# A paged-attention layer: new keys transposed on VectorE and moved through DRAM, score columns ordered by chunk, one mask buffer

## The chip, the cores and the metric

The kernel runs on one core of a Trainium2 chip. The metric is the device time of one execution in microseconds; three executions of the kernel before took 1196.81, 1202.33 and 1201.21 us, with a median of 1201.21. A further execution was taken under the hardware profiler; every line of a profile quoted here comes from such an execution.

## The reference

All data are fp32. There are B = 8 sequences of S = 128 tokens and width 512. Two layers with residuals are computed:

```python
x = x + einsum('bsi,boi->bso', x, weight[adapter_ids])       # one 512 x 512 adapter per sequence
q = rope(rmsnorm(x @ Wq.T, q_norm_w))    # 32 query heads of D = 128
k = rope(rmsnorm(x @ Wk.T, k_norm_w))    # 8 key heads: the "new keys"
v = x @ Wv.T
k_all = concat(k_cache[block_table], k)  # 512 cached keys, then 128 new ones
v_all = concat(v_cache[block_table], v)
scores = einsum('bqhd,bkhd->bhqk', q, k_all) * SCALE   # each key head serves 4 query heads
scores = where(valid, scores, -1e30)     # cached keys from cache_seqlens on are masked; new ones never
o = einsum('bhqk,bkhd->bqhd', softmax(scores), v_all)
x = x + o @ Wo.T
```

So every query head of every sequence has a 128 x 640 score matrix, and there are 256 of them.

## The kernel before, in words

The work is cut into 32 steps, `steps = [(g, b) ...]`: four groups g of 8 query heads with 2 key heads each (G = 4, GQ = 8, GK = 2), and in each group the eight sequences b. A step has eight heads h; heads 0 to 3 use the first key head (j = 0) and the first half of the queries (n = 0), heads 4 to 7 the second ones. The order of instructions on each engine is the order in which the Python code issues them: the tile scheduler is put into manual mode, and the pools (`work` with one buffer, `news` with three, and so on) only decide which buffer an allocation waits for.

For a head the loop issues two score matmuls into one PSUM buffer of two (`sc`, line 1031): 512 columns and 128 columns[...]. Line 1041 (VectorE) adds the mask while it copies the scores to `p` and keeps the minimum; line 1057 (ScalarE) takes the exponential with its sum; line 1098 (VectorE) inverts the sum; line 1105 (GpSimd, called POOL in the profile) scales `p`. `turn_p` (line 871, VectorE) transposes `p` in blocks of 32 x 32, `send` writes it to DRAM (`xp`), and `receive` reads it back as `pT`, which completes the transposition of 128 x 640.

Between the heads stand the pieces of `main`, matmuls of 512 columns: the projections of the next step (`pj_kv`, `pj_q`, from `project`), the values of the step before (`o`, from `values`), the output projection (`out`), and in group 0 the adapters (`y`). A planner deals them out: a matmul costs `UNIT = 0.86`, a TensorE transposition `TR = 0.11`, and each head gets an even share of what is left. Transpositions on TensorE that must stand at a certain head are entered in `turns_at` by `at(step, head, early, function, count)`; an early one is issued before the head's exponential, another after the pieces of the head.

Cached keys come by indirect DMA, are transposed by VectorE in `send_k` (line 786), go to DRAM (`xk`) and come back as `kT[j]` in `receive_k` (line 799). Queries go the same way in `send_q`: VectorE transposition `tq` (line 807), DRAM (`xq`, line 809), and back as `qT[n]` (line 816). All of these DMAs are issued on SP's queue in program order.

The new keys go another way. `rotate` normalises and rotates them into the tile `k` (for steps after the first GpSimd writes them with the features permuted, line 671, so that their feature order is that of the cached keys); `norm_scales` scales them on VectorE (line 695). `turn_k(i, j)` then transposes one key head on TensorE (`kt`, line 763), and ScalarE copies the result into the fifth chunk of `kT[j]` (line 764). This happens twice a step: for j = 0 at head 6 of the step before, and for j = 1 at head 2 of its own step. Queries of the first and last steps, listed in `by_pe`, are turned on TensorE in a like way (`turn_q`).

The tile `kT[j]` is laid out as (a, c, i): a is the key number modulo 4, c the chunk of 128 keys, i the index within. The score columns have this order, so both score matmuls read contiguous columns. The mask has the same order, in two buffers that steps use in turn (line 632).

Of the kernel before, what the change touches and what calls it, by code (L numbers as in the profile page):

```python
# [11 lines left out]
FP = mybir.dt.float32  # L12
# [6 lines left out]
P = 128  # L19
# [33 lines left out]
def lora_then_paged_attention(  # L53
# [155 lines left out]
    for a in range(4):  # L209
# [7 lines left out]
        )  # L217
        nc.gpsimd.memset(quad[rows, :], float(a))

    key_no = const.tile([P, 4, LC, Q4], FP, name="key_no")  # L220
    nc.gpsimd.iota(
        key_no,
        pattern=[[1, 4], [P, LC], [4, Q4]],
        base=0,
        channel_multiplier=0,
        allow_small_or_imprecise_dtypes=True,
    )
    mhalf = const.tile([P, GQ + GK], FP, name="mhalf")
    nc.gpsimd.memset(mhalf, -0.5)
    masks = [const.tile([P, 4, NC, Q4], FP, name=f"mask_{n}") for n in range(2)]  # L230
    for m in masks:
        nc.gpsimd.memset(m[:, :, LC, :], 0.0)


    lora_ix = const.tile([P, B], I32, name="lora_ix")
# [21 lines left out]
    for i, (g, b) in enumerate(steps):  # L257
        if i == 0:
            at(i, 2, False, lambda: turn_q(0, 1))
            at(i, 7, False, lambda: turn_q(1, 0))  # L260
            for n, h in enumerate((7, 8, 9, 10)):
                at(i, h, False, lambda n=n: turn_weights(("o1", 0, n)))
        if i == last:
            at(i - 1, 6, False, lambda: turn_q(last, 0))
            at(i, 2, True, lambda: turn_q(last, 1))
        at(i, 2, True, lambda i=i: turn_k(i, 1), 1)
        if i < last:
            at(i, 6, False, lambda i=i: turn_k(i + 1, 0), 1)
        if g == 0 and b + 2 < B:
            at(i, 0, True, lambda b=b: turn_x(b + 2))  # L270
            for c in range(KC):
                at(i, c if i else c + 2, False, lambda b=b, c=c: turn_lora(b + 2, c))
            at(i, 8 if i else 9, True, lambda b=b: turn_x1(b + 2))
    for turns in turns_at.values():
        turns.sort(key=lambda t: not t[0])

# [111 lines left out]
    def rope_angles():  # L388
        nc.vector.tensor_copy(row_f[:, 0:B], row_i[:, 0:B])
        row = spread(0)  # L390
        nc.vector.tensor_copy(len_f, row[:, 0:B])
        par_f = rope["par"] = const.tile([P, 1], FP, name="par_f")
        nc.vector.tensor_copy(par_f, par)
        pos = const.tile([P, B], FP, name="pos")
        nc.vector.tensor_scalar(pos, len_f, par_f, None, ALU.add)
        def temp(tag):
            t = work.tile([P, 4, D], FP, tag=tag, name=f"rope_{tag}")
            return t.rearrange("p h (u d) -> p (h u) d", u=2)

        ang, turns, sin, cos = temp("q0"), temp("q1"), temp("tq0"), temp("sw")  # L400
        nc.vector.tensor_tensor(
            ang,
            pos.unsqueeze(2).to_broadcast([P, B, H2]),
            row[:, at_ivf : at_ivf + H2].unsqueeze(1).to_broadcast([P, B, H2]),
            ALU.mult,
        )
        nc.vector.tensor_scalar(turns, ang, 1.0 / (2 * math.pi), ROUND, ALU.mult, ALU.add)
        nc.vector.tensor_scalar(turns, turns, ROUND, None, ALU.subtract)
        for part in (TWO_PI_1, TWO_PI_2, TWO_PI_3):
            nc.vector.scalar_tensor_tensor(  # L410
                out=ang, in0=turns, scalar=-part, in1=ang, op0=ALU.mult, op1=ALU.add
            )
        nc.vector.tensor_scalar(ang, ang, PI_BELOW, -PI_BELOW, ALU.min, ALU.max)
        rope.update(ang=ang, sin=sin, cos=cos)
# [185 lines left out]
    class Step:  # L600
        def __init__(self):
            self.kT, self.qT, self.q, self.pT, self.oT = {}, {}, {}, {}, {}
            self.scaled = set()

    st = [Step() for _ in steps]
# [22 lines left out]

    def make_mask(i):

        b = steps[i][1]
        nc.vector.tensor_scalar(
            masks[i % 2][:, :, 0:LC, :], key_no, len_f[:, b : b + 1], FAR, ALU.is_ge, ALU.mult
        )


# [2 lines left out]
    def rotate(i, y, dst, ss, table, n, between=None):  # L639
# [9 lines left out]
        sw = work.tile([P, 4, D], FP, tag="sw", name=f"sw_{i}_{table}")  # L649


        turned_order = i > 0 and (table == 1 or (i, n) in by_pe)
        cw = dst
        if turned_order and table:
            cw = sw[:, 2 : 2 + heads, :]
        elif turned_order:
            cw = work.tile([P, 4, D], FP, tag=f"tq{n}", name=f"cw_{i}_{n}")
        nc.vector.tensor_tensor(
            cw, t, CW[:, table, b, :].unsqueeze(1).to_broadcast([P, heads, D]), ALU.mult
        )  # L660
# [20 lines left out]
    def norm_scales(i, n, width):  # L681

        s = st[i]
        ss = s.ss[n]
        rs = small.tile([P, 6], FP, tag=f"rs{n}", name=f"rs_{i}_{n}")
        nc.gpsimd.tensor_scalar(ss[:, 0:width], ss[:, 0:width], EPS, 1.0, ALU.add, ALU.mult)
        nc.gpsimd.tensor_tensor(rs[:, 0:width], ss[:, 0:width], mhalf[:, 0:width], ALU.pow)  # L687

        def rest():
            for h in range(4):  # L690
                q = s.q[n][:, h, :]
                nc.scalar.activation(q, q, AF.Identity, scale=rs[:, h : h + 1])  # L692
            if n == 0:
                for j in range(GK):
                    nc.vector.tensor_scalar(
                        s.k[:, j, :], s.k[:, j, :], rs[:, 4 + j : 5 + j], None, ALU.mult
                    )
            s.scaled.add(n)
            if (i, n) not in by_pe:
                later.append(lambda: send_q(i, n))  # L700

        pending.append(rest)

    def project(i, what):
# [1 line left out]
        s = st[i]  # L706

        def after_kv(y):
            s.k = work.tile([P, GK, D], FP, tag="k", name=f"k_{i}")
            s.vn = news.tile([P, GW], FP, tag="vn", name=f"vn_{i}")  # L710
            s.ss = [
                small.tile([P, 6], FP, tag=f"ss{n}", name=f"ss_{i}_{n}") for n in range(2)
# [1 line left out]

            def rest():
                nc.scalar.copy(s.vn, y[:, GW : 2 * GW])
                rotate(i, y, s.k, s.ss[0][:, 4:6], 1, 0)

            pending.append(rest)

        def after_q(n):
            def after(y):
                s.q[n] = work.tile([P, 4, D], FP, tag=f"q{n}", name=f"q_{i}_{n}")

                def rest():
                    rotate(
                        i,
                        y,
                        s.q[n],
                        s.ss[n][:, 0:4],  # L730
                        0,
                        n,
# [14 lines left out]
    def turn_kc(i, j, copy=None):  # L747

        s = st[i]
        s.kT[j] = work.tile([P, 4, NC, Q4], FP, tag=f"kT{j}", name=f"kT_{i}_{j}")  # L750
        t = ps_mm.tile([P, HID], FP, tag="mm", name=f"kct_{i}_{j}")
        t = t.rearrange("d (c a i) -> d c a i", c=LC, a=4)
        for c in range(LC):
            nc.tensor.transpose(
                t[:, c, :, :].rearrange("d a i -> d (a i)"), s.kc[:, c, j * D : (j + 1) * D], ident
            )
        (copy or nc.scalar.copy)(s.kT[j][:, :, 0:LC, :].rearrange("d a c i -> d c a i"), t)

    def turn_k(i, j, copy=None):
        s = st[i]  # L760
        t = ps_mm.tile([P, HID], FP, tag="mm", name=f"kt_{i}_{j}")
        t = t[:, 0:P].rearrange("d (i a) -> d i a", a=4)
        nc.tensor.transpose(t.rearrange("d i a -> d (i a)"), s.k[:, j, :], ident)  # L763
        (copy or nc.scalar.copy)(s.kT[j][:, :, LC, :].rearrange("d a i -> d i a"), t)  # L764

    def turn_q(i, n, copy=None):
        s = st[i]
# [27 lines left out]

    def receive_k(i, j):
        s = st[i]
        s.kT[j] = work.tile([P, 4, NC, Q4], FP, tag=f"kT{j}", name=f"kT_{i}_{j}")
        nc.sync.dma_start(
            out=s.kT[j][:, :, 0:LC, :].rearrange("d b c k -> d b (c k)"),  # L800
            in_=s.xk[:, :, j, :].rearrange("b d x -> d b x"),
        )

    def send_q(i, n):
        s = st[i]
        tq = work.tile([P, 4, 4, Q4], FP, tag=f"tq{n}", name=f"tq_{i}_{n}")
        nc.vector.transpose(tq, s.q[n].rearrange("p h (a d) -> p a h d", a=4))
        xq = xch.tile([4, P, 4, Q4], FP, tag=f"xq{n}", name=f"xq_{i}_{n}")
        nc.sync.dma_start(
            out=xq.rearrange("b (i a) h q -> (b i) (a h q)", a=4),  # L810
            in_=tq.rearrange("p a h q -> p (a h q)"),
# [2 lines left out]
        def receive():  # L814
            s.qT[n] = work.tile([P, 4, 4, Q4], FP, tag=f"qT{n}", name=f"qT_{i}_{n}")
            nc.sync.dma_start(
                out=s.qT[n].rearrange("d b h q -> d b (h q)"),
                in_=xq.rearrange("b d h q -> d b (h q)"),
            )

        to_read.append((now[0], 0, receive))

# [45 lines left out]
    def turn_p(u, r):  # L868
        if r == 0:
            u.tp = turned.tile([P, 4, REP, QK], FP, tag="tp", name=f"tp_{u.i}_{u.j}")  # L870
        nc.vector.transpose(u.tp[:, :, r, :], u.p.pop(r).rearrange("q (a k) -> q a k", a=4))  # L871

    def turn_p_pe(u, r):

# [97 lines left out]
        turn_lora(1, c, on_vec if c % 2 else on_act, True)  # L972
    gather_lora(2)
    turn_q(0, 0, on_act)
    turn_k(0, 0, on_act)
    for _ in range(3):
        load_next()

# [2 lines left out]
    for i, (g, b) in enumerate(steps):  # L981
# [38 lines left out]
        for h in range(8):  # L1020
# [6 lines left out]
                )  # L1027

            sc = ps_sc.tile([P, 1024], FP, tag="sc", name=f"sc_{i}_{h}")
            for lo, hi in ((0, L), (L, LA)):  # L1030
                nc.tensor.matmul(  # L1031
                    sc[:, lo:hi],
                    lhsT=s.qT[j][:, r, :, :].rearrange("d h q -> d (h q)"),
                    rhs=s.kT[j].rearrange("d a c i -> d (a c i)")[:, lo:hi],
                    start=True,
                    stop=True,
                )
# [3 lines left out]
            nc.vector.tensor_tensor_reduce(  # L1041
                out=p,
                in0=sc[:, 0:LA],
                in1=masks[i % 2].rearrange("p a c i -> p (a c i)"),
                scale=1.0,
                scalar=3.0e38,
                op0=ALU.add,
# [52 lines left out]
            if i == last and j == 1:  # L1100

                unit.p[r] = probs.tile([P, LA], FP, tag="p", name=f"pk_{h}")
                p = p.rearrange("q (a c i) -> q a c i", a=4, c=NC)
                q = unit.p[r].rearrange("q (c i a) -> q a c i", a=4, c=NC)
            nc.gpsimd.tensor_scalar(q, p, unit.rc[:, one], 1.0, ALU.mult, ALU.mult)  # L1105
            prev = (unit, r)

# [75 lines left out]
```

## Time and profile before

| what | value |
|---|---|
| runs, median (lowest to highest) | 1201.21 us (1196.81 to 1202.33) |
| profiled execution, its own time | 1197.03 us |
| its span, first to last instruction | 1194.7 us |
| busy: TensorE, its weight loads, VectorE, ScalarE, GpSimd | 99%, 48%, 61%, 44%, 56% |
| granted TensorE clock | 1.0 |
| DMA queues, share of 16 engines | 59.6% (SP), 12.4% (ScalarE), 10.1% (GpSimd) |
| moved by DMA | 328.02 MB in 187148 packets |

The page names groups by line, engine and operation, as "out<-in", with partitions x elements, the count, the busy time in us and the mean duration of one in ns, and after a bar the idle time ahead of it on its engine and who ended it. PE is TensorE, PEld its weight loads, DVE VectorE, ACT ScalarE. A matmul of fp32 data appears as two passes, each with its own record, and a TensorE transposition as one. The records of neighbouring passes overlap in time, so that the distance between two starts, not the duration, is what a pass takes of TensorE.

### The profile page before, as it was taken

To read this page: it belongs to the slowest core of one execution; us is meant where nothing else is said; L and a number is where in the kernel's file an instruction comes from. 1 tells how busy PE (TensorE), PEld (TensorE's weight loads), DVE (VectorE), ACT (ScalarE), POOL (GpSimd) and SP (SyncE) were. 2 spreads that over 40 slices of the span, in tenths; PEclk is the share of its full clock that TensorE was granted. 3 is DMA by queue.
4 is the path that set the end of the run, shared out by engine and by line. 5 is a ranking of instruction groups with operands and counts; after the bars stand their busy time and mean duration, and the time that the engine had idled before them with its cause. 6 is when DMAs were issued, how large, how long until landed. Compare 5 with 4: busy or idle time off the path is not lost.

```text
span 1194.7 us, 12971 instructions
## 1 busy us (share of the span) xinstructions
PE 1178.0 (99%) x3412; PEld 576.4 (48%) x3412; DVE 733.6 (61%) x1675; ACT 531.5 (44%) x1648; POOL 674.9 (56%) x781
## 2 busy tenths in 40 slices
PE   7899999999999999999999999999999999999998
PEld 4554455454444444444444444444444444444454
DVE  5566656665566666766566676666657655565651
ACT  4564444444444444444444444444444444444432
POOL 5566455545566556555655556565556556655540
PEclk9999999999999999999999999999999999999999
DMA  8388788877988988888998998888898987777761
GB/s 290 110 278 273 261 292 293 275 261 246 309 289 301 334 303 300 294 270 300 296 303 280 340 313 298 298 278 300 267 319 277 303 285 264 243 255 242 260 222 60
DMA packets 187148, 328.02 MB, mean 275 GB/s; under 512 B 13124, under 2 KB 106052, under 8 KB 178116
## 3 DMA queue, kind: packets, MB, share of 16 engines
q1 hardware_dynamic: 124272, 239.23, 59.6%
q10 hardware_dynamic: 49524, 48.12, 12.4%
q0 software_dynamic: 13280, 39.86, 10.1%
q8 instruction: 27, 0.44, 0.2%
q14 instruction: 45, 0.37, 0.1%
HBM read 195.04 MB, written 132.12 MB: 274 GB/s over the span
## 4 chain that ended last, share of the span: by engine, by line
PE 97%; DMA 1%; ACT 1%; DVE 0%; POOL 0%; issue 0%; ACTq 0%; DVEq 0%; POOLq 0%
PE o L559 23%; PE sc L1031 23%; PE pj_q L559 18%; PE out L559 18%; PE pj_kv L559 9%; PE y L559 2%; PE lw L474 1%; DMA w_q<-xw_q 1%; PE x L474 1%; PE kt L763 1%; PE wt_q L492 0%; PE wt_kv L492 0%; PE qt L772 0%; PE wt_o L492 0%; PE pt L881 0%
## 5 line engine op out<-in xcount | busy, mean ns | idle before, releaser
L1041 DVE CUSTOM_DVE_ANT_0 p<-sc,mask 128x640 f32<-128x640 f32 x256 | 210.9, 824 | 400.5 <-PE sc L1031 400.4
L1057 ACT ACTIVATE p<-p,mn 128x640 f32<-128x640 f32 x256 | 211.6, 827 | 324.6 <-DVE mn L1041 322.4
L1031 PE MATMUL sc<-kT,qT 128*128 128x512 f32 (+1 forms) x1024 | 318.4, 433 | 1.1 <-ACT kT L764 0.8
L1105 POOL TENSOR_SCALAR p<-p,rc 128x640 f32<-128x640 f32 x252 | 201.9, 801 | 183.0 <-DVE rc L1098 181.0
L1031 PEld LDWEIGHTS sc<-kT,qT 128*128 128x128 f32 x1024 | 189.9, 190 | 226.4 <-issue 206.0
L559 PE MATMUL pj_q<-w_q,x1T 128*128 128x512 f32 x512 | 236.9, 593 | 1.4 <-ACT w_q L493 0.7
L559 PE MATMUL o<-pT,vc 128*128 128x512 f32 x512 | 236.9, 593 | 0.0
L559 PE MATMUL out<-w_o,oT 128*128 128x512 f32 (+1 forms) x528 | 234.9, 580 | 0.9 <-ACT oT L838 0.7
L871 DVE STREAM_TRANSPOSE tp<-p 128x640 f32<-128x640 f32 x252 | 211.0, 837 | 4.9 <-POOL p L1105 4.7
L610 POOL DMA_INDIRECT kc<-in_L_cond_k_cache_dram,key_ix x128 | 130.8, 1022 | 32.7 <-issue 32.5
L610 POOL DMA_INDIRECT vc<-in_L_cond_v_cache_dram,val_ix x128 | 127.9, 999 | 31.0 <-issue 30.8
L692 ACT ACTIVATE q<-q,rs 128x128 f32<-128x128 f32 x256 | 81.9, 390 | 139.1 <-POOL q L679 134.5
L559 PEld LDWEIGHTS out<-w_o,oT 128*128 128x128 f32 x528 | 95.7, 190 | 93.5 <-issue 89.9
L559 PEld LDWEIGHTS pj_q<-w_q,x1T 128*128 128x128 f32 x512 | 92.4, 190 | 93.8 <-issue 91.4
L559 PEld LDWEIGHTS o<-pT,vc 128*128 128x128 f32 x512 | 91.9, 190 | 88.6 <-issue 81.3
L559 PE MATMUL pj_kv<-w_kv,x1T 128*128 128x512 f32 x256 | 116.6, 593 | 0.7 <-ACT x1T L476 0.7
L671 POOL TENSOR_TENSOR k<-sw 128x256 f32<-128x256 f32 x31 | 22.9, 739 | 157.1 <-PE kt L763 133.4
L679 POOL TENSOR_TENSOR q<-q,sw 128x512 f32<-128x512 f32 x59 | 74.7, 1266 | 45.0 <-DVE sw L662 44.9
L646 ACT ACTIVATE sq<-pj_q 128x128 f32<-128x128 f32 x256 | 70.8, 277 | 50.4 <-PE pj_q L559 41.5
L687 POOL TENSOR_TENSOR rs<-ss,mhalf 128x6 f32<-128x6 f32 x64 | 77.6, 1212 | 5.3
L559 PEld LDWEIGHTS pj_kv<-w_kv,x1T 128*128 128x128 f32 x256 | 45.9, 190 | 45.6 <-issue 44.7
L559 PE MATMUL o<-pT,vn 128*128 128x512 f32 x128 | 65.4, 593 | 0.0
(123 smaller groups left out, 873.6 us busy)
## 6 DMA issues: line engine op xcount, KB each, us to landing
xp<-tp SPq DMA_DIRECT2D x63, 1280.0 KB, 5.9
pT<-xp SPq DMA_DIRECT2D x63, 1280.0 KB, 7.0
xk<-tk SPq DMA_DIRECT2D x31, 512.0 KB, 7.5
kT<-xk SPq DMA_DIRECT2D x62, 256.0 KB, 6.6
xq<-tq SPq DMA_DIRECT2D x59, 256.0 KB, 4.6
qT<-xq SPq DMA_DIRECT2D x59, 256.0 KB, 5.2
st_q<-in_L_cond_Wq_dram ACTq DMA_DIRECT2D x24, 256.0 KB, 5.3
xw_q<-tw_q ACTq DMA_DIRECT2D x24, 256.0 KB, 4.4
```

The source lines that it names most:

```text
L474: nc.tensor.transpose(t[:, j, :], blk, ident)
L559: nc.tensor.matmul(y[0], lhsT=lhsT, rhs=rhs, start=(k == 0), stop=(k == len(pieces) - 1))
L610: nc.gpsimd.indirect_dma_start(out=dst[:, c, :], out_offset=None, in_=src, in_offset=bass.IndirectOffsetOnAxis(ap=rows[:, g, at : at + 1], ...
L646: nc.scalar.activation(sq, t[:, h, :], AF.Square, scale=float(D) ** -0.5, accum_out=ss[:, h : h + 1])
L679: add.tensor_tensor(dst, cw, sw[:, 0:heads, :], ALU.add)
L687: nc.gpsimd.tensor_tensor(rs[:, 0:width], ss[:, 0:width], mhalf[:, 0:width], ALU.pow)
L692: nc.scalar.activation(q, q, AF.Identity, scale=rs[:, h : h + 1])
L871: nc.vector.transpose(u.tp[:, :, r, :], u.p.pop(r).rearrange("q (a k) -> q a k", a=4))
L1031: nc.tensor.matmul(sc[:, lo:hi], lhsT=s.qT[j][:, r, :, :].rearrange("d h q -> d (h q)"), rhs=s.kT[j].rearrange("d a c i -> d (a c i)")[:, ...
L1041: nc.vector.tensor_tensor_reduce(out=p, in0=sc[:, 0:LA], in1=masks[i % 2].rearrange("p a c i -> p (a c i)"), scale=1.0, scalar=3.0e38, op0 ...
L1057: nc.scalar.activation(p, p, AF.Exp, bias=unit.mn[:, one], scale=-1.0, accum_out=unit.sm[:, one])
L1105: nc.gpsimd.tensor_scalar(q, p, unit.rc[:, one], 1.0, ALU.mult, ALU.mult)
```

## The change

The new keys of a step are no longer transposed on TensorE, but for steps 0, 1 and the last. They are written beside the first four query heads, into a tile `q0` of 4 + GK heads; `send_q` transposes all six heads in one VectorE instruction and writes them to DRAM in one DMA, and a further DMA brings the keys back as `kn`, a tile of its own with three buffers. `kT[j]` keeps the four cached chunks alone. In steps 0, 1 and last, `turn_k` transposes both key heads on TensorE into one PSUM tile and copies them into `kn` at once.

The score columns are now ordered (c, a, i), chunk first. The 512-column matmul reads `kT[j]` in that order, as runs of 32 floats. The 128-column matmul reads `kn`, whose keys lie in natural order within each block b of 32, as (a, b, m): every fourth float. The mask and the key numbers follow the new order, the transposition of `p` reads runs of 32 floats and writes as before, and there is one mask buffer. For the last sequence of group 0 the entry of `turn_x1` is moved from the head after step 5 to its last head.

```diff
-    key_no = const.tile([P, 4, LC, Q4], FP, name="key_no")
+    key_no = const.tile([P, LC, 4, Q4], FP, name="key_no")
...
-    masks = [const.tile([P, 4, NC, Q4], FP, name=f"mask_{n}") for n in range(2)]
+    mask = const.tile([P, NC, 4, Q4], FP, name="mask")
...
         if i == 0:
             at(i, 2, False, lambda: turn_q(0, 1))
+            at(i, 6, False, lambda: turn_k(1), 2)
             at(i, 7, False, lambda: turn_q(1, 0))
...
         if i == last:
+            at(i - 1, 6, False, lambda: turn_k(last), 2)
             at(i - 1, 6, False, lambda: turn_q(last, 0))
             at(i, 2, True, lambda: turn_q(last, 1))
-        at(i, 2, True, lambda i=i: turn_k(i, 1), 1)
-        if i < last:
-            at(i, 6, False, lambda i=i: turn_k(i + 1, 0), 1)
...
-            at(i, 8 if i else 9, True, lambda b=b: turn_x1(b + 2))
+            at(i, (7 if b + 3 == B else 8) if i else 9, True, lambda b=b: turn_x1(b + 2))
...
-        turned_order = i > 0 and (table == 1 or (i, n) in by_pe)
+        turned_order = i > 0 and (i, n) in by_pe
...
-                    nc.vector.tensor_scalar(
-                        s.k[:, j, :], s.k[:, j, :], rs[:, 4 + j : 5 + j], None, ALU.mult
-                    )
+                    k = s.q[0][:, 4 + j, :]
+                    nc.vector.tensor_scalar(k, k, rs[:, 4 + j : 5 + j], None, ALU.mult)
...
-            s.k = work.tile([P, GK, D], FP, tag="k", name=f"k_{i}")
+            s.q[0] = work.tile([P, 4 + GK, D], FP, tag="q0", name=f"q_{i}_0")
...
-    def turn_k(i, j, copy=None):
-        s = st[i]
-        t = ps_mm.tile([P, HID], FP, tag="mm", name=f"kt_{i}_{j}")
-        t = t[:, 0:P].rearrange("d (i a) -> d i a", a=4)
-        nc.tensor.transpose(t.rearrange("d i a -> d (i a)"), s.k[:, j, :], ident)
-        (copy or nc.scalar.copy)(s.kT[j][:, :, LC, :].rearrange("d a i -> d i a"), t)
+    def new_keys(i):
+        s = st[i]
+        if s.kn is None:
+            s.kn = news.tile([P, 4, GK, Q4], FP, tag="kn", name=f"kn_{i}")
+        return s.kn
+
+    def turn_k(i, copy=None):
+        s = st[i]
+        t = ps_mm.tile([P, HID], FP, tag="mm", name=f"kt_{i}")
+        for j in range(GK):
+            nc.tensor.transpose(t[:, j * P : (j + 1) * P], s.q[0][:, 4 + j, :], ident)
+        (copy or nc.scalar.copy)(
+            new_keys(i).rearrange("d b j q -> d j b q"),
+            t[:, 0 : GK * P].rearrange("d (j b q) -> d j b q", j=GK, b=4),
+        )
...
     def send_q(i, n):
         s = st[i]
-        tq = work.tile([P, 4, 4, Q4], FP, tag=f"tq{n}", name=f"tq_{i}_{n}")
+        heads = 4 if n else 4 + GK
+        tq = work.tile([P, 4, heads, Q4], FP, tag=f"tq{n}", name=f"tq_{i}_{n}")
         nc.vector.transpose(tq, s.q[n].rearrange("p h (a d) -> p a h d", a=4))
-        xq = xch.tile([4, P, 4, Q4], FP, tag=f"xq{n}", name=f"xq_{i}_{n}")
+        xq = xch.tile([4, P, heads, Q4], FP, tag=f"xq{n}", name=f"xq_{i}_{n}")
...
-                in_=xq.rearrange("b d h q -> d b (h q)"),
+                in_=xq[:, :, 0:4, :].rearrange("b d h q -> d b (h q)"),
             )
+            if n == 0:
+                nc.sync.dma_start(
+                    out=new_keys(i).rearrange("d b j q -> d b (j q)"),
+                    in_=xq[:, :, 4 : 4 + GK, :].rearrange("b d j q -> d b (j q)"),
+                )
...
-        nc.vector.transpose(u.tp[:, :, r, :], u.p.pop(r).rearrange("q (a k) -> q a k", a=4))
+        nc.vector.transpose(
+            u.tp[:, :, r, :].rearrange("q a (c i) -> q a c i", c=NC),
+            u.p.pop(r).rearrange("q (c a i) -> q a c i", c=NC, a=4),
+        )
...
-            for lo, hi in ((0, L), (L, LA)):
+            for lo, hi, keys in (
+                (0, L, s.kT[j].rearrange("d a c i -> d c a i")),
+                (L, LA, s.kn[:, :, j, :].rearrange("d b (m a) -> d a b m", a=4)),
+            ):
                 nc.tensor.matmul(
                     sc[:, lo:hi],
                     lhsT=s.qT[j][:, r, :, :].rearrange("d h q -> d (h q)"),
-                    rhs=s.kT[j].rearrange("d a c i -> d (a c i)")[:, lo:hi],
+                    rhs=keys,
...
-                in1=masks[i % 2].rearrange("p a c i -> p (a c i)"),
+                in1=mask.rearrange("p c a i -> p (c a i)"),
```

More of the change, by code (lines that the diff above doesn't have):

```diff
@@ L218, in lora_then_paged_attention @@
         nc.gpsimd.memset(quad[rows, :], float(a))
-    key_no = const.tile([P, 4, LC, Q4], FP, name="key_no")
+    key_no = const.tile([P, LC, 4, Q4], FP, name="key_no")
     nc.gpsimd.iota(
         key_no,
-        pattern=[[1, 4], [P, LC], [4, Q4]],
+        pattern=[[P, LC], [1, 4], [4, Q4]],
         base=0,
@@ L229, in lora_then_paged_attention @@
     nc.gpsimd.memset(mhalf, -0.5)
-    masks = [const.tile([P, 4, NC, Q4], FP, name=f"mask_{n}") for n in range(2)]
-    for m in masks:
-        nc.gpsimd.memset(m[:, :, LC, :], 0.0)
+    mask = const.tile([P, NC, 4, Q4], FP, name="mask")
+    nc.gpsimd.memset(mask[:, LC, :, :], 0.0)
     lora_ix = const.tile([P, B], I32, name="lora_ix")
@@ L396, in temp @@
         def temp(tag):
-            t = work.tile([P, 4, D], FP, tag=tag, name=f"rope_{tag}")
-            return t.rearrange("p h (u d) -> p (h u) d", u=2)
+            n = 4 + GK if tag in ("q0", "tq0") else 4
+            t = work.tile([P, n, D], FP, tag=tag, name=f"rope_{tag}")
+            return t[:, 0:4, :].rearrange("p h (u d) -> p (h u) d", u=2)
         ang, turns, sin, cos = temp("q0"), temp("q1"), temp("tq0"), temp("sw")
@@ L602, in __init__ @@
             self.kT, self.qT, self.q, self.pT, self.oT = {}, {}, {}, {}, {}
+            self.kn = None
             self.scaled = set()
@@ L632, in make_mask @@
         nc.vector.tensor_scalar(
-            masks[i % 2][:, :, 0:LC, :], key_no, len_f[:, b : b + 1], FAR, ALU.is_ge, ALU.mult
+            mask[:, 0:LC, :, :], key_no, len_f[:, b : b + 1], FAR, ALU.is_ge, ALU.mult
         )
@@ L656, in rotate @@
         elif turned_order:
-            cw = work.tile([P, 4, D], FP, tag=f"tq{n}", name=f"cw_{i}_{n}")
+            cw = work.tile([P, 4 if n else 4 + GK, D], FP, tag=f"tq{n}", name=f"cw_{i}_{n}")
+            cw = cw[:, 0:4, :]
         nc.vector.tensor_tensor(
@@ L716, in rest @@
                 nc.scalar.copy(s.vn, y[:, GW : 2 * GW])
-                rotate(i, y, s.k, s.ss[0][:, 4:6], 1, 0)
+                rotate(i, y, s.q[0][:, 4 : 4 + GK, :], s.ss[0][:, 4:6], 1, 0)
             pending.append(rest)
@@ L722, in after @@
             def after(y):
-                s.q[n] = work.tile([P, 4, D], FP, tag=f"q{n}", name=f"q_{i}_{n}")
+                if n:
+                    s.q[n] = work.tile([P, 4, D], FP, tag=f"q{n}", name=f"q_{i}_{n}")
                 def rest():
@@ L728, in rest @@
                         y,
-                        s.q[n],
+                        s.q[n][:, 0:4, :],
                         s.ss[n][:, 0:4],
@@ L749, in turn_kc @@
         s = st[i]
-        s.kT[j] = work.tile([P, 4, NC, Q4], FP, tag=f"kT{j}", name=f"kT_{i}_{j}")
+        s.kT[j] = work.tile([P, 4, LC, Q4], FP, tag=f"kT{j}", name=f"kT_{i}_{j}")
         t = ps_mm.tile([P, HID], FP, tag="mm", name=f"kct_{i}_{j}")
@@ L756, in turn_kc @@
             )
-        (copy or nc.scalar.copy)(s.kT[j][:, :, 0:LC, :].rearrange("d a c i -> d c a i"), t)
-    def turn_k(i, j, copy=None):
+        (copy or nc.scalar.copy)(s.kT[j].rearrange("d a c i -> d c a i"), t)
+    def new_keys(i):
         s = st[i]
-        t = ps_mm.tile([P, HID], FP, tag="mm", name=f"kt_{i}_{j}")
-        t = t[:, 0:P].rearrange("d (i a) -> d i a", a=4)
-        nc.tensor.transpose(t.rearrange("d i a -> d (i a)"), s.k[:, j, :], ident)
-        (copy or nc.scalar.copy)(s.kT[j][:, :, LC, :].rearrange("d a i -> d i a"), t)
+        if s.kn is None:
[10 more added lines that the diff above has]
+        )
     def turn_q(i, n, copy=None):
@@ L797, in receive_k @@
         s = st[i]
-        s.kT[j] = work.tile([P, 4, NC, Q4], FP, tag=f"kT{j}", name=f"kT_{i}_{j}")
+        s.kT[j] = work.tile([P, 4, LC, Q4], FP, tag=f"kT{j}", name=f"kT_{i}_{j}")
         nc.sync.dma_start(
-            out=s.kT[j][:, :, 0:LC, :].rearrange("d b c k -> d b (c k)"),
+            out=s.kT[j].rearrange("d b c k -> d b (c k)"),
             in_=s.xk[:, :, j, :].rearrange("b d x -> d b x"),
@@ L974, in lora_then_paged_attention @@
     turn_q(0, 0, on_act)
-    turn_k(0, 0, on_act)
+    turn_k(0, on_act)
     for _ in range(3):
@@ L1102, in lora_then_paged_attention @@
                 unit.p[r] = probs.tile([P, LA], FP, tag="p", name=f"pk_{h}")
-                p = p.rearrange("q (a c i) -> q a c i", a=4, c=NC)
-                q = unit.p[r].rearrange("q (c i a) -> q a c i", a=4, c=NC)
+                p = p.rearrange("q (c a i) -> q c a i", a=4, c=NC)
+                q = unit.p[r].rearrange("q (c i a) -> q c a i", a=4, c=NC)
             nc.gpsimd.tensor_scalar(q, p, unit.rc[:, one], 1.0, ALU.mult, ALU.mult)
```

## The prediction

> **What bounds the kernel now.** I read the page's chain of waits first: who holds the end.
>
> ```profile
> PE 97%; DMA 1%; ACT 1%; DVE 0%; POOL 0%; issue 0%; ACTq 0%; DVEq 0%; POOLq 0%
> PE o L559 23%; PE sc L1031 23%; PE pj_q L559 18%; PE out L559 18%; PE pj_kv L559 9%; PE y L559 2%; PE lw L474 1%; DMA w_q<-xw_q 1%; PE x L474 1%; PE kt L763 1%; PE wt_q L492 0%; PE wt_kv L492 0%; PE qt L772 0%; PE wt_o L492 0%; PE pt L881 0%
> ```
>
> TensorE alone. Its own waits, asked for next, add up to 13.4 us in the whole span, 11.3 of them in the first 75 us; the steady part keeps 0.7 us of pj_kv for the copy into x1T and 0.5 and 0.2 us of pj_q where a new group's weights arrive. So a TensorE instruction taken out is worth its slot, one that gets longer costs its lengthening, and work on other engines counts only once TensorE has to wait for it. A busy PE is not the slot, since matmuls overlap; the slot is read from the timeline of TensorE, as the distance of starts:
>
> ```profile
> 620.59 2.74 PE L559 MATMUL out<-w_o,oT 128*128 128x512 f32 x6
> 623.17 0.27 PE L763 MATMUL kt<-ident,k 128*128 128x128 f32 x1
> 623.28 1.25 PE L1031 MATMUL sc<-kT,qT 128*128 128x512 f32 x4
> 624.36 3.60 PE L559 MATMUL out<-w_o,oT 128*128 128x512 f32 x8
> ```
>
> The x4 of sc are one head: a 512-column and a 128-column matmul, two passes each. Six 512-column passes take 623.17 - 620.59 = 2.58 us, 0.43 each; the head takes 624.36 - 623.28 = 1.08, so its 128-column passes have (1.08 - 0.86) / 2 = 0.107 to 0.11; the kt transposition 0.11. That is 0.84 ns a column in each. I use 0.1075.
>
> The third view is the groups with their shapes kept apart, for the price of a read or a write that steps over 16 bytes:
>
> ```profile
> L1031 PE MATMUL sc<-kT,qT 128*128 128x128 f32 x512 | 98.3, 274 | 0.0
> L763 PE MATMUL kt<-ident,k 128*128 128x128 f32 x64 | 17.4, 273 | 0.0
> ...
> L807 DVE STREAM_TRANSPOSE tq<-q 128x512 f32<-128x512 f32 x59 | 39.6, 670 | 0.0
> L786 DVE STREAM_TRANSPOSE tk<-kc 128x512 f32<-128x512 f32 x62 | 39.1, 670 | 0.0
> L506 DVE STREAM_TRANSPOSE tw_q<-st_q 128x512 f32<-128x512 f32 x24 | 25.5, 1061 | 0.0
> ...
> L584 DVE TENSOR_TENSOR acc<-y,acc 128x512 f32<-128x512 f32 x8 | 8.8, 1101 | 1.0 <-PE y L559 1.0
> ...
> L764 ACT COPY kT<-kt 128x128 f32<-128x128 f32 x64 | 24.7, 386 | 21.2 <-PE kt L763 20.6
> ```
>
> tq and tk read runs of 32 floats; tw_q, the same instruction and size, reads every fourth float: 1061 against 670 ns, 0.76 ns more an element. acc<-y (every fourth float of acc) stands at 1101 against 686 for the plain acc add: 0.81. ScalarE's kT copy reads PSUM at every fourth float: 386 against 277 for sq on 128 contiguous elements, 0.85 more. All three engines fall to about half their rate per element.
>
> [...] For TensorE's streamed operand no run here shows it: every matmul of before reads runs of 32 floats or longer. [...]
>
> **The change part by part.**
>
> Removed on TensorE: kt goes from 64 transpositions to 6 (the first, second and last step keep two each). 58 x 0.1075 = 6.2 us, all on the path. The copies behind them (58 x 0.39 us, ScalarE, 44% busy) are worth nothing.
>
> Moved: the turning of x1 for the last batch comes one head earlier (eighth head of step 5, before an output matmul and a score pair), so its copy hides: the 0.7 us wait goes. Its source is finished heads before.
>
> Step 0: both transpositions and one copy of 256 columns now stand ahead of the first score, where TensorE waits 0.84 us for the kT copy. The new copy reads PSUM contiguously, as ScalarE's vn copy of 256 columns does at 372 ns, and the old one took 386: only the second slot stays, +0.1 (that it leaves its later place is in the 58).
>
> Rest of the planner: the turns' cost is gone, so matmul pieces shift by at most one between heads (one o piece per step moves from the fifth head to the sixth); no piece is added: 0.
>
> Added on TensorE: nothing in count, but the 128-column score matmul, 256 of them in two passes, now streams kn in the order (a, b, m), every fourth float[...]. The 512-column one streams kT as (c, a, i), runs of 32 floats; o and out already stream such runs at the same 593 and 592 ns, so that is 0. The cost of the first, from both sides: 0 if TensorE absorbs it; 0.76 to 0.98 ns an element if it behaves as the others (the upper from POOL's pk, 1428 against 801 ns for 640 elements): 98 to 125 ns a pass, x 512 = 50 to 64 us. A gain is excluded, the columns are the same. I take a halved rate, one more slot per pass: 512 x 0.1075 = 55.0 us. The reason is that a pass already consumes one float in 0.84 ns, ScalarE's rate and faster than VectorE's 1.04[...]; POOL's k add (L671), at 2.9 ns an element, is the only one here that strides freely (739 against 719 ns). Against it: TensorE's fetch may be built otherwise.
>
> VectorE: tq of the first half grows from 512 to 768 columns, by 256 x 1.31 ns (from 837 against 670 for 128 more columns) = 0.34 us, 29 times. The p transposition reads runs of 32 floats, as tk does: unchanged. The mask compare writes contiguously: unchanged or shorter; with one buffer it is queued on VectorE between the last head's score read and the next head's, so order alone protects it, with no wait. VectorE is 61% busy, and TensorE never waits for its reading of sc in the steady part: 0. Queued behind the longer tq are the reciprocal and the next score read; 0.34 us there reaches TensorE only through the two score buffers, a head (some 4 us) later.
>
> POOL: the k add waited for kt to free the key tile (133 us in 23 waits) and blocked the queue; that goes, and what follows on POOL comes sooner. POOL is not on the path: 0.
>
> SP and the DMA engines: xq grows to 384 KB, and one issue (kn, 128 KB, 256-byte runs) follows each qT in SP's queue, 29 of each. Behind it stands the next probabilities' xp, for which SP waits for VectorE anyway; an issue takes about 0.36 us. Engines: 29 x 512 packets at no more than the 28 ns of 512-byte packets plus longer xq packets make about 3 points on 82%. kn lands at most about 1.5 us after qT; of the 20 landings of the first-half qT that the trace pairs, the shortest is 1.2 us ahead of its first score, the median 6.7. So one or two late arrivals of under 1 us are possible: 0 in the sum, up to 1.5 in the range.
>
> Sum: 1194.7 - 6.2 - 0.7 + 0.1 + 55.0 = 1242.9 us of span. The profiled execution took 1197.0, 2.3 more than its span: 1245.2. It lies 4.2 under the median of the runs, 1201.2, from which the same sum gives 1249.4. I take the middle, 1247.3; given this case, 1240 to 1257.
>
> **The rivals.**
>
> The stride is free. For it: [...]that TensorE's fetch is shown by no row. Then +48.2 turns into -6.8: 1190.2 from the profiled execution, 1194.4 from the median, with late landings 1190 to 1197. This ends on the other side; it decides if a pass lengthens by less than 6.8 us / 512 = 13 ns. 0.40.
>
> The stride costs a part[...]. At half the penalty 27.5 - 6.8 = +21: about 1222. 0.06.
>
> kn comes late at every step, because the same transfers wait in SP's queue and the engines stand at 80 to 90%. Against it the 6.7 us of median slack. Past that slack, each microsecond costs 29 us: 1 us late makes 1201.2 - 6.8 + 29 = 1223 with a free stride. 0.03.
>
> That the transpositions do not go is excluded: the instruction order has 6.
>
> **How the numbers follow.** The halved rate has 0.51, the largest, so 1247.3 is the forecast. The free stride must stay in the range: 1191 to 1257, which leaves out only the outermost of both. A measurement of this kernel tells about 0.5% (6 us) from no change. The halved rate, the part and the late kn are slower: 0.60. The free stride gains 6.8 with the bound at 6.0, and a little more counted from the profiled execution: 0.25 faster, 0.15 same.
>
> **What would show it.** By the shapes: kt 6 instead of 64; the 128-column sc row, now from kn, at some 380 instead of 274 ns, and a head's x4 taking 1.29 instead of 1.08 us from its start to the next group's. A step without lora (34.6 us from head to head) would go to about 36.1; with a free stride to 34.4. PE's waits should keep no line that names kn, nor the 0.7 us of pj_kv; tq at about 1.0 us. The prediction is wrong if the kn passes keep 0.11 us starts, or if TensorE starts to wait for kn or pT.

## The result, and the profile after

The changed kernel takes 1245.94 us (median of six runs, 1244.58 to 1248.04); beside it the kernel before took 1197.68 us (1196.81 to 1202.33). The ratio is 1.0396, with a 95% interval of 1.0374 to 1.0417: 4% slower. The profiled execution took 1244.58 us and its span is 1242.8 us; the prediction's sum for the span was 1242.9.

The chain of waits of the changed kernel:

```profile
PE 98%; DMA 1%; ACT 0%; DVE 0%; POOL 0%; issue 0%; ACTq 0%; DVEq 0%; POOLq 0%
PE sc L1056 27%; PE o L558 22%; PE pj_q L558 18%; PE out L558 17%; PE pj_kv L558 9%; PE y L558 2%; PE lw L473 1%; DMA w_q<-xw_q 1%; PE x L473 1%; PE wt_q L491 0%; PE wt_kv L491 0%; PE qt L784 0%; PE wt_o L491 0%; PE pt L903 0%; PE spread L383 0%
```

TensorE still holds the end. The score matmuls have gone from 23% of the span to 27%, and kt is no longer in the chain. The timeline of TensorE in group 1:

```profile
641.86 1.02 PE L1056 MATMUL sc<-kT,qT 128*128 128x512 f32 x2
642.72 0.60 PE L1056 MATMUL sc<-kn,qT 128*128 128x128 f32 x2
643.14 2.75 PE L558 MATMUL out<-w_o,oT 128*128 128x512 f32 x6
```

A head now shows as two rows, since its second matmul reads another tile. The two 512-column passes keep 0.43 us each (642.72 - 641.86 = 0.86). The two 128-column passes take 643.14 - 642.72 = 0.42 together, 0.21 each, where they had 0.11. The groups by shape, of TensorE, VectorE and GpSimd:

```profile
L1056 PE MATMUL sc<-kT,qT 128*128 128x512 f32 x512 | 261.7, 593 | 0.7 <-ACT qT L785 0.7
...
L1056 PE MATMUL sc<-kn,qT 128*128 128x128 f32 x512 | 154.2, 389 | 0.0
...
L772 PE MATMUL kt<-ident,q 128*128 128x128 f32 x6 | 1.1, 273 | 0.0
...
L821 DVE STREAM_TRANSPOSE tq<-q 128x768 f32<-128x768 f32 x29 | 27.2, 937 | 0.0
...
L681 POOL TENSOR_TENSOR q<-q,sw 128x256 f32<-128x256 f32 x30 | 21.7, 725 | 88.7 <-DVE sw L664 88.7
```

The score row on kT is unchanged to the nanosecond, though it now reads runs of 32 floats; the one on kn went from 274 to 389 ns. 58 transpositions are gone. GpSimd's key add (last row) no longer waits for kt, only for VectorE, and this shortened nothing. Where the next groups' query weights (the tile `w_q`) come in, TensorE waits 0.3 us for their transfer; it never waits for kn, and the 0.7 us of pj_kv is gone.

The length of a step, from the first score matmul of a step to that of the next, in groups 1 to 3 away from the changes of group, is 34.62 us before and 36.15 after. Two transpositions saved take off 0.22, so the sixteen kn passes of a step, with what they do to the passes behind them, added 36.15 - 34.40 = 1.75 us, 0.109 for each.

### The profile page after: what moved, and what is told of

Same layout as the page of the kernel before. It is cut to its first block, busy times and chain, and to the rows that moved or that the text cites. A ratio compares the mean times of both kernels' runs of the same rounds, so it can differ in the third digit from the quotient of the medians.

```text
span 1242.8 us, 12645 instructions
## 1 busy us (share of the span) xinstructions
PE 1226.9 (99%) x3354; PEld 617.9 (50%) x3354; DVE 741.0 (60%) x1675; ACT 516.7 (42%) x1587; POOL 674.3 (54%) x780
## 4 chain that ended last, share of the span: by engine, by line
PE 98%; DMA 1%; ACT 0%; DVE 0%; POOL 0%; issue 0%; ACTq 0%; DVEq 0%; POOLq 0%
PE sc L1056 27%; PE o L558 22%; PE pj_q L558 18%; PE out L558 17%; PE pj_kv L558 9%; PE y L558 2%; PE lw L473 1%; DMA w_q<-xw_q 1%; PE x L473 1%; PE wt_q L491 0%; PE wt_kv L491 0%; PE qt L784 0%; PE wt_o L491 0%; PE pt L903 0%; PE spread L383 0%
## 5 line engine op out<-in xcount | busy, mean ns | idle before, releaser
L1056 PE MATMUL sc<-kT,qT 128*128 128x512 f32 x512 | 261.7, 593 | 0.7 <-ACT qT L785 0.7
L681 POOL TENSOR_TENSOR q<-q,sw 128x512 f32<-128x512 f32 (+1 forms) x89 | 96.7, 1086 | 120.6 <-DVE sw L664 118.1
L1056 PEld LDWEIGHTS sc<-kn,qT 128*128 128x128 f32 x512 | 97.3, 190 | 122.4 <-issue 122.4
L1056 PE MATMUL sc<-kn,qT 128*128 128x128 f32 x512 | 154.2, 389 | 0.0
L558 PEld LDWEIGHTS out<-w_o,oT 128*128 128x128 f32 x528 | 101.6, 193 | 95.3 <-issue 85.4
L1056 PEld LDWEIGHTS sc<-kT,qT 128*128 128x128 f32 x512 | 94.9, 190 | 108.8 <-issue 105.9
L558 PEld LDWEIGHTS pj_q<-w_q,x1T 128*128 128x128 f32 x512 | 98.9, 194 | 95.9 <-issue 91.1
L558 PEld LDWEIGHTS o<-pT,vc 128*128 128x128 f32 x512 | 98.6, 194 | 90.6 <-issue 87.5
L558 PEld LDWEIGHTS pj_kv<-w_kv,x1T 128*128 128x128 f32 x256 | 49.5, 194 | 46.3 <-issue 45.3
```

The source lines that it names most:

```text
L558: nc.tensor.matmul(y[0], lhsT=lhsT, rhs=rhs, start=(k == 0), stop=(k == len(pieces) - 1))
L681: add.tensor_tensor(dst, cw, sw[:, 0:heads, :], ALU.add)
L1056: nc.tensor.matmul(sc[:, lo:hi], lhsT=s.qT[j][:, r, :, :].rearrange("d h q -> d (h q)"), rhs=keys, start=True, stop=True,)
```

## The experiments

Each kernel below has as many TensorE instructions as the kernel which it edits. Where no interval is given, the time is that of one execution, and one of the kernel before on the same chip took 1198.37 us (beside the last one 1199.26).

### kn read in runs

```diff
-                (L, LA, s.kn[:, :, j, :].rearrange("d b (m a) -> d a b m", a=4)),
+                (L, LA, s.kn[:, :, j, :]),
```

> The changed kernel with one edit: the 128-column score matmul streams kn as it lies, in runs of 32 floats, so that the new keys' score columns keep the order of the keys and are not reordered (that part of the computation is left out). The DMAs, the tiles and the instruction count are those of the changed kernel. Theory (the stride of 16 bytes halves the rate of these 512 passes): a kn pass takes 0.107 us from start to start instead of 0.215, the span falls by 55 us from 1242.8 to 1187.9, which is 6.8 us under the kernel before. Rival (kn comes late or its own tile costs, whatever the order of reading): the span stays within 5 us of 1242.8.

Measured: 1199.89 us, span 1198.1. The group by shape and the waits of TensorE, with their total, their number and the longest in us:

```profile
L1056 PE MATMUL sc<-kn,qT 128*128 128x128 f32 x512 | 98.4, 274 | 0.0
```

```profile
PE spread L383 <- DVE row_f L387: 6.1, 1, 6.1
PE pj_q L558 <- DMA w_q<-xw_q: 4.3, 3, 2.1
```

To set beside them, the waits of pj_q for a new group's weights in the kernel before, then in the changed kernel:

```profile
PE pj_q L559 <- issue: 0.5, 1, 0.5
PE pj_q L559 <- DMA w_q<-xw_q: 0.2, 1, 0.2
```

```profile
PE pj_q L558 <- DMA w_q<-xw_q: 0.3, 1, 0.3
```

The pass is back at 274 ns, and a step away from the group changes takes 34.40 us, so the order of reading alone is what had made the kn passes longer. The rival, that kn comes late or that its tile costs whatever the order, falls. But the span is 10.2 us over what was expected. 4.6 us are in the start: the first score matmul of the kernel stands at 45.09 us here and at 40.48 in the changed kernel, of which the last section speaks. The rest is at the three changes of group: the steps in which the new group's first query projection is due took 35.97, 35.60 and 38.43 us instead of 34.40, 6.8 us more, because the weights w_q were not there. The same three steps of the kernel before exceed its 34.62 by 1.2 us, and those of the changed kernel its 36.15 by 0.9, so that 5.9 of the 6.8 are new.

### Every second and every eighth float

```diff
-                (L, LA, s.kn[:, :, j, :].rearrange("d b (m a) -> d a b m", a=4)),
+                (L, LA, s.kn[:, :, j, :].rearrange("d b (m a) -> d a b m", a=2)),
```

and the same with `a=8`.

> The changed kernel with the 128-column score matmul streaming kn at every second float, 8 bytes apart (the new keys' columns are in another order than the values need, so the reordering is not done rightly). Theory[...]: the kn pass is back at 0.107 us, span about 1188. Rival (any stride over one element costs): 0.16 to 0.215 us a pass, span 1215 to 1243.

> The changed kernel with the 128-column score matmul streaming kn at every eighth float, 32 bytes apart (again another column order than the values need). Theory[...] the pass stays at 0.215 us and the span at 1243. Rival (the cost grows with the distance): over 0.25 us a pass, span over 1260.

Measured: 1202.70 us (span 1200.9) for every second float, 1247.84 us (span 1246.1) for every eighth. Their rows by shape, first of the one, then of the other:

```profile
L1056 PE MATMUL sc<-kn,qT 128*128 128x128 f32 x512 | 98.9, 274 | 0.0
```

```profile
L1056 PE MATMUL sc<-kn,qT 128*128 128x128 f32 x512 | 153.5, 388 | 0.0
```

At 8 bytes the pass costs nothing extra: 274 ns, as in runs. At 32 bytes it costs what 16 bytes cost, 388 against 389 ns. So the cost sets in above 8 bytes, at 16 at the latest, and is the same at 32. Where between 8 and 16 it sets in, and by what mechanism, is not shown: 12 bytes was not run. The span of the first is above the expected 1188 for the same two reasons as with kn read in runs: the start (first score at 45.31 us) and 5.0 us of waits for w_q.

### The stride alone, in the kernel before

```diff
             for lo, hi in ((0, L), (L, LA)):
+                keys = s.kT[j].rearrange("d a c i -> d (a c i)")[:, lo:hi]
+                if lo:
+                    keys = keys.rearrange("d (m x) -> d x m", x=4)
                 nc.tensor.matmul(
...
-                    rhs=s.kT[j].rearrange("d a c i -> d (a c i)")[:, lo:hi],
+                    rhs=keys,
```

> The kernel before with one edit: its second score matmul streams the same 128 columns of kT at every fourth float, 16 bytes apart (the order of these columns is changed, and with it the keys they stand for). No kn, no further DMA, 64 transpositions on TensorE as before. Theory (the stride alone is the cost): 512 passes x 0.1075 us = 55 us more, span 1194.7 + 55 = 1249.7. Rival (the cost comes from the rest of the change): span within 3 us of 1194.7.

Measured: 1254.84 us, span 1253.1, so 58.4 us more than before, with nothing else of the change in it. A step takes 36.48 us instead of 34.62: 1.86 for sixteen passes, 0.116 for each, counted as above. The row:

```profile
L1034 PE MATMUL sc<-kT,qT 128*128 128x128 f32 x512 | 157.7, 398 | 0.0
```

The stride alone makes the loss and a little more. Why a pass is 9 ns longer here (398) than on kn (389) stays open; the 128 columns lie in one contiguous piece here and in four pieces of 128 bytes there.

### Keys sorted before TensorE reads them

Here the whole change stays, with the right order of columns. VectorE sorts the keys within their block of 32 while it transposes them, in two instructions of its own, and TensorE reads runs of 8 floats. The copies of the three steps turned on TensorE write the same order (not in the lines below).

```diff
...
-        nc.vector.transpose(tq, s.q[n].rearrange("p h (a d) -> p a h d", a=4))
+        nc.vector.transpose(
+            tq[:, :, 0:4, :], s.q[n][:, 0:4, :].rearrange("p h (a d) -> p a h d", a=4)
+        )
+        if n == 0:
+            for j in range(GK):
+                nc.vector.transpose(
+                    tq[:, :, 4 + j, :].rearrange("p b (a m) -> p b m a", a=4),
+                    s.q[0][:, 4 + j, :].rearrange("p (b m a) -> p b m a", b=4, a=4),
+                )
...
-                (L, LA, s.kn[:, :, j, :].rearrange("d b (m a) -> d a b m", a=4)),
+                (L, LA, s.kn[:, :, j, :].rearrange("d b (a m) -> d a b m", a=4)),
```

> The changed kernel, whole and with the right output, with the new keys sorted on VectorE: the two key heads are transposed by two instructions of their own that write every fourth float, so that kn arrives with the keys of one remainder side by side, and the 128-column score matmul streams runs of 8 floats. Theory[...]: kn passes at 0.107 us; steps of 34.40 us in groups 1 to 3 away from the group changes, against 34.62 in the kernel before; but the weights of the next group come late as they did with kn read in runs, 1 to 4 us at each of the three group changes, so 1190 to 1199 us of span, ratio to before 0.995 to 1.002. Rival (runs of 8 are still too short): passes between 0.12 and 0.215 us, span 1195 to 1243. VectorE pays two instructions of 0.35 us instead of 0.27 us of the longer one, off the path.

Measured: 1197.01 us (median of 14) against 1199.52 (of 27) of the kernel before, ratio 0.9987 (0.9972 to 1.0003). The kn pass has 274 ns, the ordinary step 34.40 us. A pass now jumps to another piece of the tile after each eighth float, so a jump as such is not what costs. The waits of TensorE:

```profile
PE pj_q L558 <- DMA w_q<-xw_q: 6.2, 3, 2.2
PE spread L383 <- DVE row_f L387: 6.1, 1, 6.1
```

So without its stride the change is worth 6.8 us by its sum, of which the medians show 2.5, not told from nothing. What is lost is lost at the three group changes, where the next group's weights arrive too late: in the profiled execution these steps took 36.79, 36.85 and 38.36 us, 8.8 us over 34.40 together. The windows view of the kernel before shows how little reserve there is. It gives a stretch's length, the busy time and number of instructions of PE, PEld, DVE, ACT and POOL, the granted clock, the mean share of the DMA engines, and GB/s:

```profile
870.00:878.00 8.00, 8.00 (x23) 3.77 (x22) 4.27 (x11) 2.85 (x9) 3.16 (x4) 1.00 1.12 331
878.00:884.00 6.00, 6.00 (x18) 2.89 (x17) 4.40 (x11) 2.67 (x11) 3.20 (x5) 1.00 0.82 298
```

Around the third group change the DMA engines were full in the kernel before (a share of 1.12; the view adds up packets' times, so it can pass 1). Of the 24 reads of query weights the traces pair most with a landing; from issue to landing they took, in the kernel before and then with kn read in runs:

```profile
DMA to landing us min/median/max: 4.1/7.4/10.9
```

```profile
DMA to landing us min/median/max: 6.4/9.1/11.3
```

### The weights read one head earlier

The middle entry is for the query weights of the first half, `q0`: their four reads move from heads 4 to 7 of the seventh step of a group to heads 3 to 6.

```diff
-                read_at(before + 8 * (B - 2) + (2, 4, 6)[k] + n, (kind, g, n))
+                read_at(before + 8 * (B - 2) + (2, 3, 6)[k] + n, (kind, g, n))
```

> The same kernel with the new keys sorted on VectorE, and the read of the first-half query weights of the next group one head earlier. Theory (what is left of the lost gain is these weights landing after their first use): no wait of pj_q for w_q but under 0.5 us in all, span 1187 to 1191, ratio to before 0.990 to 0.995. Rival (the DMA engines are the limit, and an earlier issue only makes other transfers late): waits of the same size elsewhere, span as without the earlier read.

Measured, this edit on top of the sorted keys: 1191.14 us (median of six, 1189.54 to 1192.08), ratio 0.9932 (0.9913 to 0.9951), span 1189.1. It is the fastest here, 0.7% under the kernel before. No wait for w_q is left; the first two of the three steps take 34.40 us, the third 35.67, with 1.0 us of another wait, of o at 885.90 us. The profile puts it down to a ScalarE exponential, which o does not read. o reads `pT`, whose transfer was issued at 879.02 us, 6.9 us earlier, and the kernel before has a median of 7.0 us from issue to landing for this transfer. So it is likely that pT came late, and then the rival has a small part in it; the trace pairs no landing that would show it. Three rows of its TensorE timeline, to set beside those above:

```profile
701.73 1.02 PE L1064 MATMUL sc<-kT,qT 128*128 128x512 f32 x2
702.59 0.38 PE L1064 MATMUL sc<-kn,qT 128*128 128x128 f32 x2
702.81 3.60 PE L558 MATMUL o<-pT,vc 128*128 128x512 f32 x8
```

702.81 - 702.59 = 0.22 for the two kn passes: half of the 0.42 of the changed kernel. The sorting instructions cost VectorE 361 ns each, unseen by TensorE.

> The kernel before with the same earlier read of the query weights and nothing else. Its waits there are 0.7 us in all (0.5 at the first group change, 0.2 at the second), so at most 1 us less: ratio 0.998 to 1.001, span 1193.5 to 1195.

The same edit in the kernel before: 1197.60 us, ratio 0.9994 (0.9981 to 1.0008), span 1194.5. The earlier read alone is worth nothing that can be told; it matters only once these weights come late.

### Is it the read of kn that makes them late?

```diff
+            if n == 0:
+                kn = work.tile([P, 4, 32], FP, tag="kn", name=f"kn_{i}")
+                nc.sync.dma_start(
+                    out=kn,
+                    in_=xq.rearrange("b d h q -> d b (h q)")[:, :, 0:32],
+                )
```

> The kernel before with one more DMA after each first-half qT: it reads 512 short runs (128 bytes each, as many packets as the read of kn has) from xq into a tile that nothing uses. Score matmuls and TensorE transpositions as before. If the added transfers are what makes the next group's query weights late, pj_q waits for w_q at the group changes rise from 0.7 us to 3 us or more, span 1197 to 1200. If the lateness comes from the shorter steps instead, they stay under 1 us, span about 1194.7.

Measured: 1200.31 us, span 1198.2. The waits of pj_q here, and below them those of the changed kernel with every eighth float:

```profile
PE pj_q L559 <- DMA w_q<-xw_q: 1.6, 2, 1.3
```

```profile
PE pj_q L558 <- DMA w_q<-xw_q: 1.2, 2, 0.9
```

The first is between the two forecasts. The three steps exceed 34.62 by 2.5 us together, against 1.2 without the read and 6.8 with the whole change in runs. But the second shows how far single executions differ: with every eighth float the transfers are those of the changed kernel and a step is within 0.03 us of its 36.15, and yet the wait is 1.2 us instead of 0.3, and the three steps exceed by 2.1 instead of 0.9. So it is not shown that this read alone makes the weights later; it moves half the bytes of kn and leaves the write of xq as it was.

Other traces on record tell more. Where the steps are long, the median time of these weights from issue to landing is 7.6 us without the change's transfers (the stride alone, in the kernel before) and 8.6 with them (every eighth float); where they are short, it is 7.4 without (the kernel before) and 9.1 with (kn read in runs). The thirteen reads that have a landing in all four traces split the same way: 6.9 and 7.3 us without, 8.4 and 8.9 with. So the slower landing goes with the transfers of the change and not with the shorter steps, by one execution each; longer steps leave the weights more time. Which of the added transfers it is, the read of kn or the longer write of xq, stays open.

## Why the prediction was right

By its own steps:

- **The kn passes, +55.0 us.** The cost and its size are right. Reading in runs and the stride put into the kernel before show the cause from both sides. Per step it is 1.75 us, or 56 us over 32 steps. From start to start, in the ordinary steps, a pass on kn takes 212.8 ns where the same columns took 110.4. Some 4 of the 56 us show in the 512-column pass right behind each pair, 447.5 ns instead of 431.7; the passes after it are no longer than before. The reason given was weaker than the result. "All three engines" were two in the lines beside it, VectorE and ScalarE, and ScalarE's copy reads PSUM; of GpSimd, one instruction paid (1428 against 801 ns) and one did not (739 against 719). Nor is it "about half": by the durations given there VectorE falls to 0.63 and 0.62 of its rate and ScalarE to 0.72. It was an inference from other engines, to which the prediction itself gave a chance of 0.51; the runs have now shown for TensorE that steps of 16 and 32 bytes lengthen a pass, to 389 and 388 ns, and one of 8 does not, at 274. That the 0.84 ns a column are the reason was the author's estimate, and was not tested by itself.
- **58 transpositions, -6.2 us.** Right: 34.62 - 34.40 = 0.22 us a step, two slots.
- **x1, -0.7 us.** Right: the wait of pj_kv is gone.
- **Step 0, +0.1 us.** The first score matmul stands at 40.48 us, from 40.77: 0.3 earlier, with the query transpositions before it at 39.21 in both. TensorE still waits, 0.5 us, now for the copy of qT: its first matmul needs qT and kT alone, and the copy of the new keys hides behind it. The step overlooked that the split tile frees the first matmul.
- **VectorE, +0.34 us a transposition.** 937 ns against 670 is 0.27; the term was mis-sized, since the 256 added columns cost 1.04 ns each and not the 1.31 taken from the p transposition. Off the path, as said.
- **DMA engines, 3 points.** Their share of the span is 81.2%, of a longer span: 1009 us of engine time against 981, which is 2.4 points of the old span.
- **The sum.** 1242.9 us of span was forecast, 1242.8 measured. That the two agree to 0.1 us is luck: the six executions have spans of 1242.8 to 1246.3, and the kn passes and step 0 missed in opposite directions. The median of 1245.94 is 1.4 under the forecast of 1247.3, because the runs beside it gave the kernel before a median of 1197.68 and not 1201.21.

One step was wrong without touching the forecast: the rival of a free stride. It was priced at -6.8 us, or 1190 to 1197 us with a few late arrivals of kn. The three kernels without the cost of the stride took 1199.89, 1202.70 and, with sorted keys, 1197.01 us. TensorE never waits for kn there, but it does for w_q, 4 to 6 us in all. The step looked for the late transfer among those that the change adds, and not among those that share the DMA engines with them. The slower score matmuls of the changed kernel hide most of this: with steps longer by 1.75 us, TensorE waits 0.3 us for these weights there, and 1.2 with every eighth float.

## What to carry to other kernels

Before TensorE is given a strided operand to stream, look at the step between its elements: for fp32, 8 bytes were free here (274 ns a pass, as in runs), and 16 bytes all but doubled the pass from start to start (110 to 213 ns). A permutation that would bring in such a step belongs to an engine with time to spare, here 361 ns of VectorE for each key head. And when a change takes work off a bound engine at 99% and puts 2 to 3% more on DMA engines at over 80%, look at the stretches where these are already full, for the transfers of others that are due there.

## What had not been expected of the hardware

The pace of TensorE at the start differs from one execution to the next. The eight passes of the first adapter matmul, in the kernel before and then with kn read in runs:

```profile
15.44 3.67 PE y L559 x8
```

```profile
17.89 5.82 PE L558 MATMUL y<-wT,x1T 128*128 128x512 f32 x8 [0.88 <-DVE wT L475]
```

(The first is from the chain, the second from the timeline.) They take 1.6 times as long there, and the first score matmul came at 40.5 us to 45.3 us in the ten profiled executions. The later start goes with a later time from which the trace's record of the clock grants full speed: 11.6 us in the first, 22.2 us in the second. The changed kernel, which has the instructions of the second up to there, has full speed from 10.3 us on by that record, and its first score matmul stands at 40.48. The spread of the start is as large as what the change removes, so the spans of two single executions can be compared to no better than some 5 us; the lengths of their steps can.

A wait of about 2 us cost more than itself. In the run with kn read in runs, at the third group change:

```profile
876.47 0.38 PE L1056 MATMUL sc<-kn,qT 128*128 128x128 f32 x2
878.91 5.40 PE L558 MATMUL pj_q<-w_q,x1T 128*128 128x512 f32 x8 [2.06 <-DMA w_q<-xw_q]
```

The eight passes after the wait took 5.40 instead of 3.60 us, and the record of the granted clock shows 0.5 for 3.41 us from 879.0 us on. That is why this step lost 4.0 us and not 2.1. It does not follow every such wait. Of the nine waits for w_q in the runs with kn read in runs, with every second float and with sorted keys, four of the six of about 2 us had such a stretch behind them, each of 3.41 us, and none of the three of 1.3 us or less.
